# Attention with relative tables: where a head's value-table work, its key-table layout and its row copies stand

## The chip, the cores and the metric

The kernel runs on one core of one Trainium2 chip. The metric is the time of one execution in microseconds on the device; the median of several executions counts. TensorE, VectorE, ScalarE, GpSimd and SyncE each have an instruction stream of their own and meet through semaphores; in the views they are PE (PEld for its weight loads), DVE, ACT, POOL and SP. SPq, ACTq and POOLq are DMA issues by those engines.

## What is computed

The reference is two layers of a network on `x` of shape (4, 384, 32, 32): attention and a feed-forward with factored weights, then depthwise convolutions and a mixture of four experts. Everything is fp32. The change lies in the attention of the first layer, 8 heads of 48 features over 1024 pixels and 4 images:

```
attn = q @ k.T                                        # q is scaled, (b, h, 1024, 1024)
attn = attn + take(q @ table_k.T, idx)                # idx[i, j]: clipped (dy, dx) of pixels i and j, 15 x 15
attn = attn + take((k * scale) @ table_q.T, idx).T
attn = softmax(attn)
out  = attn @ v
wsum[i, idx[i, j]] += attn[i, j]                      # sums of the weights by offset
out  = out + wsum @ table_v
out  = out @ w_proj + b_proj
```

## The kernel before

**Stages.** A first phase normalises `x` and writes queries, keys and values to DRAM (to about 240 us of the span), the attention phase runs the 8 heads one after another (to about 1560 us), and a third phase does all the rest (to 3159 us). Only the attention phase is touched. Its matmuls, copies and DMAs are pinned: each engine executes them in the order in which the Python program writes them down.

**One head** consists of two parts.

*Tables.* `prepare` multiplies keys with `table_q` (tile `tabq_ps`) and queries with `table_k` (`tabk_ps`), one product of 128 x 480 for each of 32 columns of the image (480 is 15 row offsets by 32). A step handles two columns of each, the `tabq` columns four ahead of the `tabk` columns, so there are 18 steps a head. ACT copies each `tabq` product from PSUM (L314) and SP writes it to the DRAM tile `sd` (L220), from which SP loads it back transposed (`s1`; the views call it `s`). DVE transposes each `tabk` product in blocks of 32 x 32 from PSUM into `b2` (L309). `b2` is laid out `[offset, y, x]`, so a transposed column lands in words that lie 32 words (128 bytes) apart. Six steps of the next head's tables run during the last two rows of a head and after them; the other twelve follow before the head's first row.

*Rows.* For each of 32 image rows y (one row of all four images is 128 queries, by 1024 keys):

- `fetch` (L352): POOL adds `b2` and `s1` into a tile `bias` of 128 x 1024 by up to three additions; three such tiles exist. Row pairs of `s1` come by one DMA of 480 KB; two such tiles exist.
- `scores`: 16 matmuls into one of two PSUM tiles (`sc_ps`).
- `biased` (L380): DVE adds scores and bias, and takes the row minimum. It frees the `sc_ps` tile.
- `exponentials` (L390): ACT, with the row sums.
- `far_sums` (L401): three DVE reductions for the offsets beyond the window.
- `transposes` (L409): 8 on PE, and two ACT copies (L410) into `aT`.
- `windows` (L419): 4 transposes on PE; `keep_windows` (L428) copies their 128 x 512 result into `a1t`. Odd y and y = 16 are copied by ACT, the others by DVE: 17 and 15 of 32.
- after each four rows, `values`: 64 matmuls (`av_ps`) and one ACT copy (L443).

Scores run three rows ahead of the transposes, `biased` two, `far_sums` one.

*Value table.* After rows 15 and 31, `wsum @ table_v` is computed in four quarters: `value_table(g)`, 64 matmuls with weights from `tvw` and data from `a1t` into one PSUM bank (`tv_ps`), then `add_table` (L478), four DVE additions onto the head's output `o`. The quarters for rows 16 to 31 of a head stand at the start of the next head: after its first two scores come quarters 0 and 1 with their additions, then the matmuls of quarter 2, `biased` and `exponentials` of row 0, the addition and the matmuls that are left, scores of row 2, and so on (L530 to L546). `tvw` for the next use is loaded by 15 DMAs of 192 KB, one a row from row 1, and the values `vb` by 4 DMAs of 256 KB at rows 0 to 3; both are issued by ACT (`bulk`, L223), in order with its copies and exponentials. Queries (`qs`), `s1`, `sd` and the softmax denominators (`rb`) are DMAs of SP (`dma`, L220). Besides the bias, POOL scales the finished output of a half head (L490), once at each of the rows 4, 8, 20 and 24.

## Time and profile before

| | |
|---|---|
| median of 3 runs | 3158.37 us (3157.34 to 3163.52) |
| profiled execution, its own time | 3161.11 us |
| its span, first to last instruction | 3159.3 us, granted PE clock 0.970 |
| busy PE / DVE / ACT / POOL | 2975.0 / 2000.4 / 1331.1 / 1157.8 us |
| attention, first `biased` of head 4 to that of head 5 | 938.72 to 1101.99 us |

In the views, a line of a group gives source line, engine, operation, output and input tiles, shapes and count, then the busy time and the mean ns of one, then the idle time of the engine just before them and what ended it. A line of a timeline gives start, length, engine, source line and count of merged instructions, and in brackets the idle time before them. A line of a window gives the stretch, then the busy time of PE, PEld, DVE, ACT and POOL (with counts), the granted PE clock as a share of full speed, the DMA share and GB/s.

### The profile page before, as it was taken

The numbers are of one execution on the slowest core, as the hardware profiler recorded it, in microseconds if no ns is written. First come the engines' busy times: TensorE is split into PE (matmuls) and PEld (weight loads), VectorE is DVE, ScalarE is ACT, GpSimd is POOL, SyncE is SP. The second block draws the span as 40 slices with busy tenths as digits, with TensorE's granted clock in tenths as the row PEclk, the third lists the DMA queues.
The fourth block names the chain that finished last, engine by engine and source line by source line (L and its number), as shares of the span: only waits on it lengthen the run. The fifth ranks groups of instructions, "written<-read, shape, count | busy, mean of one in ns | idle before, by whom it ended". The sixth has DMA issues, their size and how long they took to land.

```text
span 3159.3 us, 63461 instructions
## 1 busy us (share of the span) xinstructions
PE 2975.0 (94%) x25591; PEld 2061.6 (65%) x25591; DVE 2000.4 (63%) x3739; ACT 1331.1 (42%) x2695; POOL 1157.8 (37%) x1100
## 2 busy tenths in 40 slices
PE   8998999999999999999878997998999999999996
PEld 4545766667676767676633374674677777778775
DVE  2227777877788787877649399998999720001101
ACT  1105656565656566565420332342342423333332
POOL 2224637372737372737410221113135232114422
PEclk9999999999999999999989998998999999999998
DMA  3796465555555555555331322351355044475852
GB/s 126 262 313 208 126 187 138 182 135 168 147 173 148 179 141 185 142 176 155 96 112 44 128 71 110 147 206 53 127 191 189 28 174 172 155 283 173 309 206 73
DMA packets 263669, 500.53 MB, mean 158 GB/s; under 512 B 135200, under 2 KB 188064, under 8 KB 255696
## 3 DMA queue, kind: packets, MB, share of 16 engines
q1 hardware_dynamic: 156528, 214.73, 21.4%
q0 software_dynamic: 43552, 228.24, 19.6%
q10 hardware_dynamic: 63296, 53.52, 7.2%
q8 instruction: 201, 3.29, 0.4%
q14 instruction: 92, 0.75, 0.1%
HBM read 543.58 MB, written 152.37 MB: 220 GB/s over the span
## 4 chain that ended last, share of the span: by engine, by line
PE 37%; DVE 10%; issue 4%; DMA 2%; ACT 1%; POOL 1%; POOLq 0%; ACTq 0%; DVEq 0%; SPq 0%
PE e_ps L1226 14%; PE y_ps L1204 14%; DVE xb L1021 7%; PE av_ps L215 1%; PE row_ps L75 1%; PE tap_ps L1065 1%; PE o_ps L966 1%; PE t_ps L409 1%; PE all_ps L105 1%; PE proj_ps L931 1%; PE xT_ps L1188 1%; PE sc_ps L215 1%; PE f_ps L962 1%; PE tv_ps L215 0%; PE u_ps L949 0%
## 5 line engine op out<-in xcount | busy, mean ns | idle before, releaser
L352 POOL TENSOR_TENSOR bias<-b,s 128x416 f32<-128x416 f32 (+24 forms) x656 | 660.4, 1045 | 525.8 <-DMA s<-sd 434.9
L1226 PEld LDWEIGHTS e_ps<-xT,w 128*128 128x128 f32 x4824 | 654.6, 193 | 229.7 <-ACT hs L972 16.1
L1226 PE MATMUL e_ps<-xT,w 128*128 128x128 f32 x4824 | 673.3, 277 | 19.8 <-DVE xb L934 8.0
L1204 PE MATMUL y_ps<-w,eh 128*128 128x384 f32 x1608 | 651.0, 490 | 6.2 <-ACT eh L1229 6.2
L1021 DVE SCALAR_TENSOR_TENSOR xb<-img,c_w,xb 128x1024 f32<-128x1024 f32 (+1 forms) x539 | 610.2, 1189 | 0.0
L1229 ACT ACTIVATE eh<-e_ps,w 128x128 f32<-128x128 f32 x804 | 294.1, 368 | 740.7 <-PE e_ps L1226 728.1
L1194 POOL DMA_INDIRECT w<-in_w,row x134 | 163.5, 1220 | 773.5 <-PE y_ps L1204 266.5
L401 DVE TENSOR_REDUCE extra<-arow 128x32 f32<-128x32 f32 (+24 forms) x768 | 380.7, 556 | 3.3 <-ACT arow L390 2.9
L390 ACT ACTIVATE arow<-arow,nm 128x1024 f32<-128x1024 f32 x256 | 297.9, 1164 | 143.0 <-DVE nm L380 135.8
L409 PEld LDWEIGHTS t_ps<-ident,arow 128*128 128x128 f32 x2048 | 223.9, 143 | 193.0 <-DVE a1t L428 68.1
L380 DVE CUSTOM_DVE_ANT_0 arow<-sc_ps,bias 128x1024 f32<-128x1024 f32 x256 | 312.2, 1220 | 35.2 <-issue 21.0
L410 ACT COPY aT<-t_ps 128x512 f32<-128x512 f32 x512 | 277.1, 594 | 134.7 <-PE t_ps L409 129.6
L1207 DVE TENSOR_TENSOR yo<-y_ps,w 128x384 f32<-128x384 f32 x67 | 37.1, 553 | 442.0 <-PE y_ps L1204 442.0
L215 PE MATMUL sc_ps<-kk,qs 48*32 48x512 f32 x4096 | 289.3, 623 | 25.4 <-DVE nm L380 23.1
L409 PE MATMUL t_ps<-ident,arow 128*128 128x128 f32 x2048 | 287.4, 284 | 13.4 <-DVE a1t L428 12.2
L215 PEld LDWEIGHTS av_ps<-aT,vb 128*64 128x64 f32 x4096 | 224.4, 137 | 56.9 <-ACT aT L410 46.9
L1204 PEld LDWEIGHTS y_ps<-w,eh 128*128 128x128 f32 x1608 | 248.2, 193 | 18.6 <-ACT eh L1229 7.8
L309 DVE STREAM_TRANSPOSE b<-tabk_ps 128x480 f32<-128x480 f32 x256 | 216.1, 1006 | 49.3 <-PE tabk_ps L215 35.7
L215 PE MATMUL av_ps<-aT,vb 128*64 128x128 f32 x4096 | 241.0, 275 | 4.6 <-DMA vb<-v_d 4.6
L215 PE MATMUL tabq_ps<-tab,kq 48*128 48x480 f32 x512 | 220.3, 579 | 2.1 <-ACT aT L410 1.4
L215 PE MATMUL tabk_ps<-tab,kq 48*128 48x480 f32 x512 | 219.3, 579 | 1.0 <-DVE b L309 1.0
L314 ACT COPY st<-tabq_ps 128x480 f32<-128x480 f32 x256 | 142.4, 561 | 74.4 <-PE tabq_ps L215 38.7
(212 smaller groups left out, 3199.4 us busy)
## 6 DMA issues: line engine op xcount, KB each, us to landing
sd<-st SPq DMA_DIRECT2D x128, 480.0 KB, 2.5
s<-sd SPq DMA_DIRECT2D x128, 480.0 KB, 4.4
xs_d<-zero POOLq DMA_DIRECT2D x8, 3072.0 KB, 12.7
tvw<-in_tv ACTq DMA_DIRECT2D x120, 192.0 KB, 3.3
y_d<-yo SPq DMA_DIRECT2D x67, 192.0 KB, 1.9
qk_d<-qk_sb POOLq DMA_DIRECT2D x48, 256.0 KB, 5.5
qs<-qk_d SPq DMA_DIRECT2D x256, 48.0 KB, 2.9
kq<-qk_d ACTq DMA_DIRECT2D x56, 192.0 KB, 3.9
```

What stands on the lines that cost most here:

```text
L215: ins = nc.tensor.matmul(*args, **kw)
L309: turn = nc.vector.transpose(b2.rearrange("p e y x -> p x (e y)")[:, i + j], ps[:, j, : SPAN * IMG])
L352: nc.gpsimd.tensor_tensor(bias[:, y0:y1, :], bass.AP(b2.tensor, b2.offset + (e * IMG + y0) * IMG, [list(b2.ap[0]), [(step * IMG + 1) * IMG ...
L380: nc.vector.tensor_tensor_reduce(s["flat"], ps.rearrange("p h n -> p (h n)"), s["bias"].rearrange("p y x -> p (y x)"), -SCALE, BIG, ALU.ad ...
L390: nc.scalar.activation(s["flat"], s["flat"], AF.Exp, bias=s["nm"], scale=-1.0, accum_out=dn[:, y % YT : y % YT + 1])
L401: pin(nc.vector.tensor_reduce(ex[:, i, :], a[:, p0:p1, :].rearrange("p y x -> p x y"), AX.X, ALU.add))
L409: pin(nc.tensor.transpose(pt[:, j, :], s["flat"][:, k0 : k0 + P], ident))
L410: pin(nc.scalar.copy(aT[:, 4 * g : 4 * g + 4, s["y"] % YB, :], pt))
L1021: nc.vector.scalar_tensor_tensor(acc[:, k, y0:y1], img[:, k, dy + y0 : dy + y1, dx : dx + IMG], w7[:, k, dy, dx : dx + 1], acc[:, k, y0:y1 ...
L1204: nc.tensor.matmul(py, hs, w[:, o : o + C], start=(ff == 0), stop=(ff == NF - 1))
L1226: nc.tensor.matmul(ph, w[:, o : o + P], xT[k][:, c, :], start=(c == 0), stop=(c == KC - 1))
L1229: nc.scalar.activation(hs, ph, AF.Gelu, bias=w[:, o : o + 1])
```

## The change

1. `b2` holds each transposed column as 480 consecutive words, columns 481 words apart. DVE now writes consecutive words; POOL, which read runs of consecutive words, now reads words that lie 481 words (1924 bytes) apart.
2. Value-table quarter 0 moves into the tables of the next head, behind the eighth of the twelve remaining steps. Quarters 1, 2 and 3 stand before, between and after the scores of rows 0 and 1. The PSUM pools of the quarters are swapped.
3. `vb` is loaded during the tables; it is still issued by ACT. `tvw` is issued by SP.
4. The first row pair of `s1` comes as two DMAs of one row each.
5. ACT copies all `a1t` rows but those with y mod 16 of 8 or 12: 28 of 32.
6. Rows 0 to 2 are ordered anew: scores and `biased` run less far ahead at first, and `windows` of row 0 waits until row 1. Rows from 3 on are as before.

```diff
-        b2 = fixed.tile([P, SPAN, IMG, IMG], F32, name="b2")
+        b2 = fixed.tile([P, IMG * PITCH], F32, name="b2")          # PITCH = SPAN * IMG + 1
                         turn = nc.vector.transpose(
-                            b2.rearrange("p e y x -> p x (e y)")[:, i + j], ps[:, j, : SPAN * IMG]
+                            b2[:, (i + j) * PITCH : (i + j) * PITCH + SPAN * IMG], ps[:, j, : SPAN * IMG]
                         )
...
+                for r, n in ((0, 2),) if y else ((0, 1), (1, 1)):
+                    dma(
+                        rows[0][:, r : r + n].rearrange("p r e x -> p r (e x)"),
...
-                            b2.tensor, b2.offset + (e * IMG + y0) * IMG,
-                            [list(b2.ap[0]), [(step * IMG + 1) * IMG, n], [1, IMG]],
+                            b2.tensor, b2.offset + e * IMG + y0,
+                            [list(b2.ap[0]), [step * IMG + 1, n], [PITCH, IMG]],
...
-            copy = nc.scalar.copy if y % 2 or y == YT else nc.vector.tensor_copy
+            copy = nc.vector.tensor_copy if y % YT in (8, 12) else nc.scalar.copy
...
-            pool, tag = (ps_o, "o") if g % 2 else (ps_t, "t")
+            pool, tag = (ps_o, "o") if g % 2 != other else (ps_t, "t")
...
-                bulk(
+                dma(
                     tvw[p : p + IMG, i // 4].rearrange("p i d -> p (i d)"),
...
-            for _ in tables:
+            parts, pieces = load_values(h), load_value_table(h)
+            for i, _ in enumerate(tables):
+                next(parts, None)
+                if n and i == 7:
+                    add_table(batch[1], 0, value_table(0, 1))
+            for _ in parts:
                 pass
             for s in blk[:3]:
                 fetch(s)
-            parts, pieces = load_values(h), load_value_table(h)
+            if n:
+                po = value_table(1, 1)
             scores(blk[0])
+            if n:
+                add_table(batch[1], 1, po)
+                po = value_table(2, 1)
             scores(blk[1])
             if n:
-                for g in range(2):
-                    add_table(batch[1], g, value_table(g))
-                po = value_table(2)
+                add_table(batch[1], 2, po)
+                po = value_table(3, 1)
             biased(blk[0])
             exponentials(blk[0])
             if n:
-                add_table(batch[1], 2, po)
-                po = value_table(3)
-            scores(blk[2])
+                add_table(batch[1], 3, po)
+            biased(blk[1])
             far_sums(blk[0])
-            biased(blk[1])
-            exponentials(blk[1])
-            if n:
-                add_table(batch[1], 3, po)
...
                 transposes(s)
-                windows(s)
-                if y == 0:
-                    scores(blk[3])
+                if y < 3:
+                    exponentials(blk[y + 1])
+                    if y == 0:
+                        scores(blk[2])
+                    if y == 1:
+                        windows(blk[0])
+                    scores(blk[y + 3])
+                    biased(blk[y + 2])
+                    far_sums(blk[y + 1])
+                    if y == 1:
+                        keep_windows(blk[0])
+                if y:
+                    windows(s)
```

## The prediction

> **What bounds it now.** I read the page first, then the timeline of the start of head 5, then windows over it, then groups by form for prices. The page's busy line and two DVE and POOL groups:

> ```profile
> PE 2975.0 (94%) x25591; PEld 2061.6 (65%) x25591; DVE 2000.4 (63%) x3739; ACT 1331.1 (42%) x2695; POOL 1157.8 (37%) x1100
> L309 DVE STREAM_TRANSPOSE b<-tabk_ps 128x480 f32<-128x480 f32 x256 | 216.1, 1006 | 49.3 <-PE tabk_ps L215 35.7 <-PE tabq_ps L215 13.5
> ```

> PE is busy nearly always, so only what PE waits for can be won, unless PE work goes away, and none does. In the rows of a head from the first `av` on PE repeats 2.48, 2.62, 2.75 and 6.12 us from scores to scores, against 2.48, 2.48, 2.48 and 6.12 in its best groups: some 0.4 us in 14. In the tables a step's products follow each other every 0.81 us on PE and `st` copies on ACT do the same; DVE needs 0.845 per transpose, a lag of 0.8 us over 24 that PE never feels (PE waits 1.0 us for L309 in the whole run). So the tables are PE's. What is left is the start of a head. Timeline, head 5, from the end of its tables:

> ```profile
> 1094.07 0.88 SPq L220 DMA_DIRECT2D s<-sd  x2
> 1094.15 1.09 PE L215 MATMUL sc_ps<-kk,qs 48*32 48x512 f32 x16
> ...
> 1096.52 7.59 PE L215 MATMUL tv_ps<-a1t,tvw 128*48 128x64 f32 x256
> ...
> 1098.03 12.40 POOL L352 TENSOR_TENSOR bias<-b,s 128x224 f32<-128x224 f32 x10 [49.72 <-DMA s<-sd]
> 1098.63 1.58 DVE L478 TENSOR_TENSOR oT<-tv_ps,oT 48x128 f32<-48x128 f32 x4 [3.19 <-issue]
> ...
> 1101.99 1.23 DVE L380 CUSTOM_DVE_ANT_0 arow<-sc_ps,bias 128x1024 f32<-128x1024 f32 x1
> ...
> 1107.87 1.09 PE L215 MATMUL sc_ps<-kk,qs 48*32 48x512 f32 x16 [0.94 <-DVE nm L380]
> ...
> 1110.64 1.96 PE L215 MATMUL sc_ps<-kk,qs 48*32 48x512 f32 x16 [1.69 <-DVE nm L380]
> ...
> 1112.13 0.68 DVE L428 COPY a1t<-a_ps 128x512 f32<-128x512 f32 x1
> ```

> The reader is to see that DVE starts 4.5 us after the tables end and is then busy without a gap, and that PE twice waits for `biased` to free a score tile. The windows show a second loss:

> ```profile
> 1106.00:1110.00 4.00, 1.90 (x22) 0.57 (x20) 3.88 (x9) 2.15 (x4) 4.00 (x4) 1.00 0.21 51
> 1110.00:1114.00 4.00, 3.36 (x23) 1.70 (x24) 4.00 (x10) 1.60 (x4) 2.95 (x3) 0.50 0.62 138
> ```

> PE is under half busy, and then its clock is granted at 0.50. DVE, not PE, is late there, so this costs little now. The first `av` (rows 0 to 3 are through) starts 27.8 us after the tables' end in head 5; over heads 1 to 7 the mean is 27.9, in head 0 it is 23.2 and the `av` is cut by a wait for `vb`.

> **Part 2 and 6, the start.** I lay the new DVE order over the durations of this timeline, T = 0 at the end of the tables. A quarter's matmuls take 7.6/4 = 1.9 us, 16 scores 1.05, an addition of a quarter 1.6, `biased` 1.15 until the next DVE instruction, `far_sums` 1.75 falling to 1.55.
> PE: quarter 1 to 1.9, scores 0 to 2.95, quarter 2 to 4.9, scores 1 to 5.95, quarter 3 to 7.9. DVE: addition 1 from 2.1 to 3.7, addition 2 from 5.05 to 6.7. Bias of row 0: the `s` DMA is issued at 0 as now; now it lands after 3.96 us, 480 KB at the 300 GB/s of this phase are 1.6 us, so half of it (part 4) saves 0.8, POOL starts at 3.2 and needs 2.6 a row (660 us over 256 rows): ready at 5.8. So `biased` 0 starts at 6.75, with addition 2 last, then without a gap addition 3, `biased` 1 at 9.45, 2 at 12.3, 3 at 15.1, 4 at 17.75, 5 at 20.4, done 21.6. ACT keeps pace: exponentials 0 end at 9.3, 1 at 12.4, 2 at 15.5, 3 at 19.0, each needed by DVE or PE no earlier. Scores 7 wait for `biased` 5 and end at 22.7; the first `av` starts there. Quarter 0 went ahead of T: plus 1.9 PE. 27.9 − 22.7 − 1.9 = 3.3 us a head, **23 us** for 7 heads. The gain is DVE's: addition 0 (1.6) and two row copies (0.7 each) leave this stretch.
> Quarter 0 in the tables: PE pauses 1.9 us there, DVE adds for 1.6, so DVE's lag doesn't grow, and two score tiles hold four transposes. Uncovered it would cost the 1.6.
> Head 0 has no quarters. `biased` 0 comes 0.8 us sooner, POOL still paces rows 1 and 2, two row copies leave DVE: scores of row 7 about 1.5 us sooner; and `av` no longer waits for `vb` (scores 7 to scores 8 take 10.3 us there instead of 6.1): **5.6 us**. Heads 1 and 2 show the same wait with 0.9 each: **1.8**.

> **Part 3.** `vb` in the tables: ACT has 0.25 us free between copies, an issue takes 0.33, four steps later it is caught up. 1 MB more among 480 KB each 1.62 us: 736 KB a step ask for 450 GB/s where 419 is the most that the DMA view shows in a slice (head 0's tables), so `sd` falls back by some 0.6 us and has eight steps to catch up. Zero, with 0.6 a head if not. `tvw`: 15 issues of 0.33 leave ACT (5.0 us a head) and stand in SP's queue behind `qs` and `s1`; needed at row 16, the last is issued at row 15, lands after 3.3. Queued behind it on SP: `s1` of the next pair, needed two rows later. Zero.

> **Part 5.** 11 copies a head at 0.585 go to ACT: 6.4 us, 1.4 net of `tvw`. DVE loses 11 of 0.68. PE's 0.4 us in 14 is half a wait for DVE's copies (L409 on L428, at y = 11 0.7 us), and an ACT copy stands behind a 1.2 us exponential: rows 4 to 15 gain some 0.2 a group, rows 17 to 31, where `tvw` was not, lose 0.2 to 0.3. Zero, ends −1 and +1 us a head.

> **Part 1.** Two prices. DVE's transpose becomes shorter: nearest rows, 1006 ns now, and 691 ns for 128x512 of consecutive words (L167): 0 to −0.35 us each. It buys nothing, as DVE is not late in the tables. POOL reads one of its two inputs at a step of 1924 bytes; the trace has no such POOL row:

> ```profile
> L352 POOL TENSOR_TENSOR bias<-b,s 128x416 f32<-128x416 f32 x176 | 189.6, 1082 | 126.6 <-DMA s<-sd 98.1 <-DVE nm L380 18.7 <-DVE extra L401 9.7
> L352 POOL TENSOR_TENSOR bias<-b,s 128x800 f32<-128x800 f32 x16 | 30.4, 1898 | 0.0
> L1047 POOL TENSOR_TENSOR w<-half,c_w 128x3136 f32<-128x3136 f32 x2 | 10.8, 5445 | 10.8 <-DVE b_first L808 10.8
> L401 DVE TENSOR_REDUCE extra<-arow 128x32 f32<-128x800 f32 x16 | 25.1, 1569 | 1.2 <-ACT arow L390 1.2
> L401 DVE TENSOR_REDUCE extra<-arow 128x32 f32<-128x512 f32 x16 | 17.4, 1087 | 0.0
> ```

> POOL pays (1898 − 1082)/384 = 2.13 ns per element; with inputs that repeat one word (L1047) 1.74. So its pattern matters: −0.4 us a row of 1024 at one end. DVE reading at a step of 128 bytes pays (1569 − 1087)/288 = 1.67, and on consecutive words (1220 for 1024, 691 for 512) 1.03: +0.64 ns, +0.65 us a row at the other. POOL is already slower per element than DVE's stepped read, so part may hide: I take +0.3. Bias 5 is ready at 3.2 + 6 × 2.9 = 20.6 where it is wanted at 20.4: **0 to 0.2 us**. At +0.65 it is 22.6, a loss of 2.2 a head, 18 in all. Later rows give POOL 14 us for four rows and at most one L490 of 1.3: 4 × 2.9 + 1.3 = 12.9 fits.
> [...]

> **The clock.** PE's waits in the new start are 7.9 to 9.3, then 0.1 to 0.65 at a time: in the worst 3.4 us PE is some 58% busy, where 48% (1.90 of 4.00) was followed by the halved clock. If it comes, transposes 0, scores 2 and 3 take 6 us instead of 3 and `biased` 2 starts 1.1 late. I count 1.1 in each of 7 heads: **−7.7**.
> [...]

> **Sum.** 23 + 5.6 + 1.8 − 7.7 = 22.7 us. Profiled execution 3161.1 − 22.7 = 3138.4; it lies 2.7 above the median of the runs shown, so 3136 for a median.

> **Rivals.** *The start stays late* (22%). One of half-rate clock over two windows, `vb` delaying `sd`, or ACT's copies costs 2 us a head more: 3136 + 16 = 3152. For it: the 0.50 lasts 6.8 us in heads 3 to 7. Against: DVE, not PE, is the chain there.
> *POOL becomes the bound* (15%), slower than before. If the column read costs +1.0 us a row (2.13 to 3.1 ns), bias 5 is ready at 24.7, 4.3 late; four rows and L490 need 15.6 of 14 us, 1.6 too much at rows 4 and 8 and 0.35 in other groups, some 3.6 until the pause at row 16. 7.9 us × 8 = 63, less the 30 won (the halved clock is covered): 3158 + 33 = 3191. POOL decides the start from +0.28 on ((20.4 − 3.2)/6 − 2.58), and the total is zero near +0.75. For it: L1047 against L352. Against: DVE's stepped price is +0.65 at most.
> *It does nothing* (3%): if `biased` 0 waited for a late `s`, as now, order on DVE would not matter: 3158.

> **Numbers.** Forecast 3136, 60%, own range 3120 to 3150 (all clocks kept and rows +1 us: −16; POOL at +0.65: +14). Range for 8 in 10: 3120 to 3168, which takes in the late start and the foot of the POOL case. The measurement tells 0.2% (6.3 us) from no change: faster is 60 + half of 22, 0.71; same 11 + 3, 0.14; slower 0.15.

> **What would show it.** Right: first `av` some 22.7 us after the tables' end; no gap on DVE from `biased` 0 to 5; PE's longest wait at `transposes` of row 0; L352 at 128x800 near 2.1 us; L309 shorter without effect. Wrong: L352 at 128x800 above 2.5 us with DVE waiting for POOL; ACT as what L409 or L419 waits for; clock 0.50 for 6.8 us in all heads; a longer pitch of `st` copies while `vb` loads.

## The result and the profile after

The changed kernel takes 3158.47 us (median of 20 runs, 3153.56 to 3164.56), the kernel before 3160.37 us (20 runs on the same chip, 3151.43 to 3170.66): a ratio of 0.9993 with an interval of 0.9983 to 1.0002, so no change. The forecast was 3136 us. The profiled execution took 3161.57 us, with a span of 3159.8 us and a granted PE clock of 0.973.

The page after, its busy line and the key column's transposes (columns as before):

```profile
PE 2972.0 (94%) x25591; PEld 2036.6 (64%) x25591; DVE 1915.7 (61%) x3651; ACT 1363.1 (43%) x2783; POOL 1288.8 (41%) x1100
L310 DVE STREAM_TRANSPOSE b<-tabk_ps 128x480 f32<-128x480 f32 x256 | 173.3, 681 | 117.5 <-PE tabk_ps L216 77.9 <-PE tabq_ps L216 17.6
```

DVE lost 85 us of work and POOL gained 131, and PE is as busy as it was. DVE now waits 77.9 us for PE in the tables, where it waited 35.7: the table steps come later than they did. The start of head 5, in the timeline after, from the end of its tables at 1101.36:

```profile
1101.42 1.27 SPq L221 DMA_DIRECT2D s<-sd  x3
1103.23 1.09 PE L216 MATMUL sc_ps<-kk,qs 48*32 48x512 f32 x16
...
1104.15 18.05 POOL L354 TENSOR_TENSOR bias<-b,s 128x224 f32<-128x224 f32 x12 [52.50 <-DMA s<-sd]
...
1106.30 1.59 DVE L480 TENSOR_TENSOR oT<-tv_ps,oT 48x128 f32<-48x128 f32 x4 [1.40 <-PE tv_ps L216]
1107.93 1.23 DVE L382 CUSTOM_DVE_ANT_0 arow<-sc_ps,bias 128x1024 f32<-128x1024 f32 x1
...
1110.49 1.09 PE L411 MATMUL t_ps<-ident,arow 128*128 128x128 f32 x8 [1.28 <-ACT arow L392]
...
1110.88 1.22 DVE L382 CUSTOM_DVE_ANT_0 arow<-sc_ps,bias 128x1024 f32<-128x1024 f32 x1
...
1120.67 1.09 PE L216 MATMUL sc_ps<-kk,qs 48*32 48x512 f32 x16 [0.81 <-DVE nm L382]
```

This is the start that was laid out: `biased` of row 0 at 6.6 us after the tables, of row 1 at 9.5, PE's longest wait at the transposes of row 0, and no gap on DVE. Windows over the end of the same head's tables, after, and before at the same place in the steps (us; busy PE, PEld, DVE, ACT, POOL; PE clock, DMA share, GB/s):

```profile
1078.00:1082.00 4.00, 4.00 (x22) 3.02 (x20) 3.37 (x6) 2.50 (x5) 0.00 (x0) 1.00 0.90 315
1082.00:1086.00 4.00, 2.61 (x14) 1.57 (x12) 1.94 (x3) 1.02 (x2) 0.00 (x0) 1.00 0.99 381
1086.00:1090.00 4.00, 4.00 (x13) 1.68 (x12) 2.05 (x3) 2.14 (x4) 0.00 (x0) 0.55 0.67 274
1090.00:1094.00 4.00, 4.00 (x56) 2.26 (x54) 1.37 (x2) 1.12 (x2) 0.00 (x0) 0.60 0.40 166
```

```profile
1075.00:1079.00 4.00, 4.00 (x22) 3.09 (x21) 3.54 (x5) 2.59 (x5) 0.00 (x0) 1.00 0.32 125
1079.00:1083.00 4.00, 4.00 (x24) 3.35 (x22) 4.00 (x6) 2.75 (x6) 0.00 (x0) 1.00 0.75 301
1083.00:1087.00 4.00, 4.00 (x23) 3.83 (x21) 4.00 (x6) 2.76 (x6) 0.00 (x0) 1.00 0.78 313
```

In these windows PE was busy throughout before, and the DMA engines were 0.78 full at most. After, they are full, PE stands still for a third of a window, and then its clock is granted at about half. The timeline of the same stretch tells why PE stood still:

```profile
1076.20 0.35 ACTq L224 DMA_DIRECT2D vb<-v_d  x1
1076.77 16.31 SPq L221 DMA_DIRECT2D sd<-st  x8
...
1077.81 0.34 ACTq L224 DMA_DIRECT2D vb<-v_d  x1
...
1079.42 0.33 ACTq L224 DMA_DIRECT2D vb<-v_d  x1
1080.72 0.56 ACT L315 COPY st<-tabq_ps 128x480 f32<-128x480 f32 x1 [0.74 <-DMA sd<-st]
1081.04 0.33 ACTq L224 DMA_DIRECT2D vb<-v_d  x1
1081.17 0.56 ACT L315 COPY st<-tabq_ps 128x480 f32<-128x480 f32 x1
...
1084.21 1.02 ACT L315 COPY st<-tabq_ps 128x480 f32<-128x480 f32 x2 [2.47 <-DMA sd<-st]
1086.36 1.02 ACT L315 COPY st<-tabq_ps 128x480 f32<-128x480 f32 x2 [1.14 <-DMA sd<-st]
```

After the third load of `vb`, ACT's copy waits for a write of `sd` to free one of the three `st` tiles, first 0.74 us, then 2.47; PE then waits for ACT. The writes are late: before, a write of `sd` in these tables landed 2.5 us after its issue; here the writes issued at 1076.77, 1078.39 and 1081.76 took 3.9, 5.7 and 6.3 us. From 420 to 1450 us of the span, the waits of the changed kernel for this chain (total, times, longest) are:

```profile
ACT st L315 <- DMA sd<-st: 33.4, 25, 3.1
PEld tabq_ps L216 <- ACT st L315: 25.4, 27, 2.8
PE tabq_ps L216 <- ACT st L315: 12.0, 9, 2.1
```

Before, ACT waited 2.6 us there. A ledger from the two traces follows, with a head cut into tables (start of the last `av` product of a head to the end of the next head's `tabk` products, mean of 7), start (to its first `av`, mean of heads 1 to 7) and rows (start of the first to start of the last `av`, mean of heads 1 to 6):

| us | tables | start | rows | sum | end of head 0's tables to last `av` |
|---|---|---|---|---|---|
| before | 20.28 | 27.86 | 116.04 | 164.2 | 1283.7 |
| after | 26.38 | 23.84 | 115.06 | 165.3 | 1285.9 |

The starts won 7 × 4.0 = 28 us, the tables lost 7 × 6.1 = 43, and the rows with head 0 won 12. Outside of this the two traces agree: to 0.4 us at the end of head 0's tables, and to 2.2 us from the last `av` to the end.

### The profile page after: what moved, and what is told of

Read it like the earlier page. It is cut to its first block, busy times and chain, and to the rows that moved or that the text cites. A ratio compares the mean times of both kernels' runs of the same rounds, so it can differ in the third digit from the quotient of the medians.

```text
span 3159.8 us, 63493 instructions
## 1 busy us (share of the span) xinstructions
PE 2972.0 (94%) x25591; PEld 2036.6 (64%) x25591; DVE 1915.7 (61%) x3651; ACT 1363.1 (43%) x2783; POOL 1288.8 (41%) x1100
## 4 chain that ended last, share of the span: by engine, by line
PE 70%; DVE 11%; issue 6%; DMA 6%; POOL 4%; ACT 2%; SPq 0%; ACTq 0%; POOLq 0%; DVEq 0%
PE e_ps L1244 14%; PE y_ps L1222 14%; PE t_ps L411 7%; PE av_ps L216 7%; DVE xb L1039 7%; PE sc_ps L216 6%; PE tabq_ps L216 5%; PE a_ps L421 3%; POOL bias L354 3%; PE qk_ps L164 2%; DMA sd<-st 2%; PE tv_ps L216 2%; DMA s<-sd 1%; PE row_ps L76 1%; PE v_ps L175 1%
## 5 line engine op out<-in xcount | busy, mean ns | idle before, releaser
L354 POOL TENSOR_TENSOR bias<-b,s 128x416 f32<-128x416 f32 (+24 forms) x656 | 793.3, 1278 | 443.6 <-DMA s<-sd 332.9
L382 DVE CUSTOM_DVE_ANT_0 arow<-sc_ps,bias 128x1024 f32<-128x1024 f32 x256 | 312.1, 1219 | 116.3 <-POOL bias L354 59.8
L411 PE MATMUL t_ps<-ident,arow 128*128 128x128 f32 x2048 | 281.0, 280 | 18.6 <-ACT arow L392 17.6
L216 PE MATMUL sc_ps<-kk,qs 48*32 48x512 f32 x4096 | 278.2, 603 | 12.8 <-DVE nm L382 12.1
L216 PE MATMUL tabq_ps<-tab,kq 48*128 48x480 f32 x512 | 238.9, 613 | 19.2 <-ACT st L315 17.0
L310 DVE STREAM_TRANSPOSE b<-tabk_ps 128x480 f32<-128x480 f32 x256 | 173.3, 681 | 117.5 <-PE tabk_ps L216 77.9
L216 PE MATMUL tabk_ps<-tab,kq 48*128 48x480 f32 x512 | 236.3, 610 | 0.0
L216 PEld LDWEIGHTS tabq_ps<-tab,kq 48*128 48x128 f32 x512 | 147.7, 298 | 84.1 <-ACT st L315 33.1
```

The costliest lines, as they stand in the source:

```text
L216: ins = nc.tensor.matmul(*args, **kw)
L310: turn = nc.vector.transpose(b2[:, (i + j) * PITCH : (i + j) * PITCH + SPAN * IMG], ps[:, j, : SPAN * IMG])
L354: nc.gpsimd.tensor_tensor(bias[:, y0:y1, :], bass.AP(b2.tensor, b2.offset + e * IMG + y0, [list(b2.ap[0]), [step * IMG + 1, n], [PITCH, IMG]],
L382: nc.vector.tensor_tensor_reduce(s["flat"], ps.rearrange("p h n -> p (h n)"), s["bias"].rearrange("p y x -> p (y x)"), -SCALE, BIG, ALU.ad ...
L411: pin(nc.tensor.transpose(pt[:, j, :], s["flat"][:, k0 : k0 + P], ident))
```

## The experiments

Two theories at first. **V**: the loads of `vb` in the tables fill the DMA engines, `sd` is late, ACT and PE wait, the clock halves. **P**: POOL's read at a step takes the gain back. All ratios are against the kernel before in the same group of runs on the same chip. The columns of the ledger are those above, from one execution of each run. That execution lies between 6.5 us below the median of its run (e8) and 7.2 us above (e4), and the stretch behind the attention, which no edit touches, differs by up to 8 us between runs of one chip. So the columns tell where time goes, and the ratios what it is worth.

| run | ratio and interval | tables | start | rows | sum | attention |
|---|---|---|---|---|---|---|
| e1 loads at the rows | 0.9960 [0.9943, 0.9978] | 22.37 | 23.66 | 116.58 | 162.6 | 1265.4 |
| e2 loads spread in the tables | 0.9995 [0.9982, 1.0008] | 22.93 | 24.93 | 115.05 | 162.9 | 1270.7 |
| e3 old layout | 0.9998 [0.9984, 1.0013] | 26.06 | 22.90 | 114.75 | 163.7 | 1275.0 |
| e4 before, loads in the tables | 1.0047 [1.0028, 1.0065] | 23.04 | 27.68 | 115.62 | 166.3 | 1295.3 |
| e5 = e1, old layout | 0.9955 [0.9937, 0.9972] | 23.07 | 23.27 | 115.88 | 162.2 | 1263.7 |
| e7 = e5, old copies | 0.9963 [0.9948, 0.9979] | 23.05 | 24.98 | 114.93 | 163.0 | 1270.8 |
| e8 = e1, two loads a row | 0.9960 [0.9945, 0.9975] | 22.35 | 25.17 | 115.05 | 162.6 | 1266.6 |
| e9 = e1, quarter 0 after | 0.9940 [0.9917, 0.9963] | 20.18 | 24.85 | 116.15 | 161.2 | 1258.5 |
| e13 quarter 0 after | 0.9973 [0.9961, 0.9985] | 23.31 | 25.16 | 114.82 | 163.3 | 1274.1 |
| e10 = e9, old layout | 0.9916 [0.9903, 0.9930] | 20.37 | 24.67 | 116.15 | 161.2 | 1257.1 |
| e11 = e9, loads a row sooner | 0.9912 [0.9898, 0.9925] | 20.20 | 24.97 | 115.82 | 161.0 | 1256.2 |
| e12 = e11, old layout | 0.9889 [0.9874, 0.9904] | 20.30 | 24.71 | 115.39 | 160.4 | 1249.3 |

**e1 and e4: the loads.** e1 is the changed kernel with the loads back at rows 0 to 3:

```diff
             for i, _ in enumerate(tables):
-                next(parts, None)
...
-            for _ in parts:
-                pass
...
                 if y + 3 < IMG:
                     fetch(blk[y + 3])
+                next(parts, None)
```

> The changed kernel with one part undone: the four loads of the values stand at rows 0 to 3 of a head again, still issued by ACT. Theory V (the loads fill the DMA engines during the tables, the sd writes fall behind, ACT and then PE wait, PE's clock halves): the tables of heads 1 to 7 lose their 4 us each, some 28 us, and 3 to 6 us come back as waits for the values in heads 0 to 2: 3134 to 3140 us, ratio to before 0.992 to 0.994, st copies 0.81 us apart throughout. Rival P (POOL's column read takes what the new start gives): within 3 us of the changed kernel, ratio 0.998 to 1.000.

e4 makes the opposite edit in the kernel before, and nothing else:

> The kernel before with one part of the change alone: the four loads of the values stand behind the table steps instead of at rows 0 to 3 (there six of 18 steps of head 0, and the first four of the last twelve of the others). Theory V: 4 us a head lost in the tables of 7 heads, 4 to 6 us won by the waits for the values in heads 0 to 2: 3178 to 3186, ratio 1.006 to 1.009. Rival P: the waits for the values go and nothing else changes, ratio 0.998 to 0.999.

ACT's wait for `sd` in the same stretch of the span is gone in e1, and is there in e4 without any other part of the change:

```profile
ACT st L315 <- DMA sd<-st: 2.9, 2, 1.6
```

```profile
ACT st L314 <- DMA sd<-st: 29.0, 25, 2.8
```

The tables fall by 4.0 us in e1 and rise by 2.8 in e4. V holds in both directions. That ACT issues the loads between its copies is not the cause: in the trace after its copies start every 0.81 us up to the third issue, and what ends its waits is a write of `sd`; and e2 below has the same issues with tables as short as e1's to 0.6 us. By time e4 lies below V's range, with an interval that reaches into it, and e1 lies between the two expectations: part of the 28 us comes back as waits for `vb` at row 4 (rows 1.5 us longer than after), and e1's tables are still 2.1 us longer than before, which is quarter 0.

**e2 and e3: spreading the loads, and the old layout alone.** e2 issues the four loads at every third step; e3 undoes the layout of `b2` in the changed kernel.

```diff
-                next(parts, None)
+                if i % 3 == 0:
+                    next(parts, None)
```

```diff
-        b2 = fixed.tile([P, IMG * PITCH], F32, name="b2")
+        b2 = fixed.tile([P, SPAN, IMG, IMG], F32, name="b2")
...
-                            b2[:, (i + j) * PITCH : (i + j) * PITCH + SPAN * IMG], ps[:, j, : SPAN * IMG]
+                            b2.rearrange("p e y x -> p x (e y)")[:, i + j], ps[:, j, : SPAN * IMG]
...
-                            [list(b2.ap[0]), [step * IMG + 1, n], [PITCH, IMG]],
+                            [list(b2.ap[0]), [(step * IMG + 1) * IMG, n], [1, IMG]],
```

> The changed kernel with the four loads of the values spread over the tables: at the first, fourth, seventh and tenth of the twelve steps instead of the first four. Theory V as a burst: 256 KB more in every third step ask for some 355 GB/s, below what the DMA engines gave (381), so the copies keep to 0.81 us and the run comes to 3132 to 3140, ratio 0.991 to 0.994. V without burst (any megabyte more is too much): ratio 0.996 to 1.000, the late steps stretched instead of the middle ones. Rival P: ratio 0.998 to 1.000.

> The changed kernel with one part undone: the key table keeps its old layout, so DVE writes words 128 bytes apart and POOL reads runs of consecutive words. Theory V: tables as in the changed kernel, POOL back to 2.58 us a row, the starts some 1 us a head shorter: 3148 to 3156, ratio 0.996 to 0.999. Rival P: DVE waited 52 us for POOL's bias in the changed kernel against 13 before; with them gone some 30 us or more are won, 3120 to 3130, ratio 0.988 to 0.991.

e2's tables are nearly cured (22.93), but its starts are 1.3 us longer than e1's: POOL's first bias of a head begins 4.5 us after the tables in place of 3.2. Part of the delay was moved to the first fetch, and by the ratio the kernel is still no faster than before, though its one traced execution, 5.6 us below the median, has an attention 13 us shorter than before. P falls with e3: POOL is back at its old price (12 additions at the start of head 5 take 14.9 us, 18.1 in the changed kernel; 10 took 12.4 before) and the starts are 0.9 us shorter, but the tables are nearly as long as after, and the time is the same. (The attention of the traced execution is 10.9 us shorter than after; of these, 7.4 are the distances of the two executions from their medians.)

**e5, e7, e8, e9: each other part, with the loads out of the tables.** e5 is e1 with e3's edit. e7 adds to it the first edit here; e8 is e1 with the second:

```diff
-            copy = nc.vector.tensor_copy if y % YT in (8, 12) else nc.scalar.copy
+            copy = nc.scalar.copy if y % 2 or y == YT else nc.vector.tensor_copy
```

```diff
-                next(parts, None)
+                if y < 2:
+                    next(parts, None)
+                    next(parts, None)
```

> The changed kernel with the values loaded at rows 0 to 3 again and the key column's table in its old order, so that DVE's transposes write with a step and POOL reads contiguously. The trace of the run with the new order and the loads at the rows gave, a head, a start 4.2 us shorter than before, tables 2.3 us longer (the quarter) and rows as long. Theory N (the new order buys nothing, its price on POOL is paid in the starts): a start some 0.8 us shorter still, as in the run with the old order alone (22.9 against 23.8 us), so a ratio of 0.992 to 0.995. Theory L (the shorter transposes make room on DVE for the quarter's adds among the tables, without them the twelve steps stretch): twelve steps of 19 us or more, ratio 0.997 to 1.000.

> As the run beside it, and with the copies of the row offsets shared between ScalarE and VectorE as before the change: what is left is the new order of a head's start, with quarter 0 among the tables, the first fetch in two parts and the pieces of the value table on SP. Theory S (the start is the whole gain, the copies are worth nothing, as the prediction took it): the same as the run with all copies on ScalarE within 0.002, that is 0.992 to 0.997. Theory C (the copies carry the rows: 114.7 to 115.0 us a head with them, 115.6 without, in the runs so far, and VectorE is freed for the start): 6 us and more lost against that run, ratio higher by 0.002 to 0.005.

> The changed kernel with the values loaded two at row 0 and two at row 1, in place of one at each of the rows 0 to 3. In the run with one a row, TensorE waited 13 us in all for these loads at the first values of a head, and the rows were 116 to 119 us long in place of 115. Theory V (the loads must only be clear of the tables and early enough for row 4): no wait for them is left, rows of 115 us, some 1.2 us a head less, ratio 0.992 to 0.995. Rival F (two loads at a row delay the fetch of the next rows' offsets, and POOL's bias with it, in the start, which is bound by them): starts of 24.5 us or more, ratio 0.997 to 1.000.

> The changed kernel with the values loaded at rows 0 to 3 and with quarter 0 of the value table after the tables again, ahead of quarter 1, not among them. Theory Z (the quarter is only moved: it took 2.24 us of the tables' pitch and frees 1.9 us and more of the start): tables of 15.4 us, starts 2 to 2.5 us longer, no difference by time within 0.0015 to the run with the quarter among the tables (0.996). Theory Q (the quarter in the tables is a gain, as the prediction took it: TensorE works there while the key column's transposes are behind): 0.998 to 1.000. Theory H (it does harm, the pause of the pitch delays the last steps and the first fetch): 0.992 to 0.994.

e5: the old layout does no harm without the loads (0.9955 against 0.9960, intervals overlap); the tables are 0.7 us longer and the starts 0.4 shorter, so neither N's gain nor L's loss is seen by time. e7: by the ratio the copies are worth 0.0008, inside the intervals, as S has it; by the medians it is 6.9 us and by the attention of the traces 7.1, in the starts (25.0 against 23.3) and not in the rows. That is open. e8: the wait for `vb` is gone and the rows are 115.05, but the start is 1.5 us longer, and from 420 to 1450 us of the span DVE waits 60.0 us for POOL's bias, 52.5 in e1, which is what F expects; the two cancel. e9 is e1 with the edit

```diff
-                if n and i == 7:
-                    add_table(batch[1], 0, value_table(0, 1))
...
-                po = value_table(1, 1)
+                p0, po = value_table(0, 1), value_table(1, 1)
...
+                add_table(batch[1], 0, p0)
```

and is the fastest of its group (3172.63 us against 3176.84 to 3183.69 of the other three). By the ledger the quarter cost the tables 2.2 us and took only 1.2 off the start, a harm of 1 us a head, as H has it; whether by H's mechanism isn't shown, and the interval of the time takes in Z as well.

**e13, e10, e11, e12: the square, and the best version.** The same edit in the changed kernel itself, with the loads still in the tables, is e13; e11 (from e9) and e12 (from e9 with the old layout, which is e10) issue the loads by

```diff
-                next(parts, None)
+                for _ in range((1, 2, 1)[y] if y < 3 else 0):
+                    next(parts, None)
```

> The changed kernel with one thing undone: quarter 0 of the value table is computed after the tables, not among them; the values are still loaded in the tables. With the run that undid the loads alone (0.996) and the run that undid both (0.994) it makes a square of two by two. Theory V (the loads in the tables are by themselves the loss, about 4 us a head, and the quarter is another 1 us): the stretch from a head's last values to the end of the next key table 24 to 24.5 us (26.4 in the changed kernel, 20.2 with both undone), the start 24.8, 1 us a head won, ratio 0.996 to 0.998. Theory I (the two together are worse than the sum: the quarter's 2.2 us of pause leaves the loads and the table's writes a longer queue, and TensorE a quiet stretch that halves its clock): the stretch 23 us as in the run of before with the loads alone, ratio 0.993 to 0.995.

> The best version so far (values at rows 0 to 3, quarter 0 after the tables: 0.994) with the key column's table in its old order. Theory N (the new order is a price on POOL and no gain without the quarter in the tables): starts of 23.9 to 24.3 us in place of 24.85, the stretch before them 20.2 to 20.4 us, ratio 0.992 to 0.994. Theory L (the new order's shorter transposes are needed): the stretch 21 us and more, ratio 0.995 or above.

> The best version so far (values at rows 0 to 3, quarter 0 after the tables) with the values at rows 0, 1, 1 and 2. In its trace TensorE waited 13 us in all for the third image's values, which had been issued 7 us ahead of their use and the fourth's 4 us ahead. Theory V: the wait goes, rows of 115.0 in place of 116.1 us, starts of 24.85 to 25 us, ratio 0.992 to 0.994. Rival F (the loads delay the row offsets that the start waits for, as two a row at rows 0 and 1 did, where the start was 25.2 in place of 23.7 us): starts of 25.8 us or more, ratio 0.994 to 0.996.

> Both at once: quarter 0 after the tables, the values at rows 0, 1, 1 and 2, the key column's table in its old order. If both are gains by their own theories they add: starts of 24 us, rows of 115 us, the stretch before 20.3 us, 159.3 us a head against 164.2 in the kernel before, 5 us a head, ratio 0.989 to 0.992. If the loads and the faster POOL meet (POOL then waits for the offsets that the loads delay), no more than the better of the two, 0.993.

By time the square adds up: with the quarter after the tables the loads cost 0.9973 − 0.9940 = 0.0033, with the quarter among them 0.9993 − 0.9960 = 0.0033, some 10 us each, give or take 8 and 6; the quarter costs 0.002 in both, clear of the noise with the loads in the tables (e13), inside it without (e9). The ledgers of single executions put the loads higher, at 15.6 and 20.5 us of attention. Theory I saw the tables rightly (23.3 us) and V the time; that the two together are worse than their sum is not shown. ACT's wait for `sd` is 31.0 us in e13, as in the changed kernel, so it does not need the quarter.

In e9 the wait that was left at the first values was this (the expectations of e8 and e11 add up the two lines and say 13 us, but they show the same waits twice, at the weights and at the products; PE's line alone is 5.8 us, and 6.1 in e1):

```profile
PEld av_ps L216 <- DMA vb<-v_d: 7.3, 6, 2.0
PE av_ps L216 <- DMA vb<-v_d: 5.8, 6, 1.8
```

With the loads at rows 0, 1, 1 and 2 no such wait is left. e12 takes 3124.53 us against 3159.73 of the kernel before, 35 us less; e11 and e10 in the same group 3132.23 and 3133.56. Each gains by time what was expected or a little more, but not where: the starts stay at 24.7 to 25.0 with either layout, where 24 was expected of the old, and e11's rows are 115.8 in place of 115.0. In e12 no half-rate clock is left in heads 1 to 7 (granted clock over the span 0.978, before 0.970), ACT waits 2.3 us for `sd`, and the groups of POOL and of the transposes are those of before:

```profile
PE 2955.1 (95%) x25591; PEld 2049.0 (66%) x25591; DVE 1954.9 (63%) x3651; ACT 1364.0 (44%) x2783; POOL 1154.1 (37%) x1100
L310 DVE STREAM_TRANSPOSE b<-tabk_ps 128x480 f32<-128x480 f32 x256 | 217.1, 997 | 56.1 <-PE tabk_ps L216 36.0 <-PE tabq_ps L216 20.2
L354 POOL TENSOR_TENSOR bias<-b,s 128x416 f32<-128x416 f32 x176 | 190.0, 1085 | 104.4 <-DMA s<-sd 82.8 <-DVE extra L403 15.4 <-DVE nm L382 6.3
```

So the version that beats both keeps the new order of the start, the copies on ScalarE, the split first fetch and `tvw` on SP, and gives up the new layout, the quarter among the tables and the loads in them. No run undoes the new order of the start, the split fetch or `tvw` on SP alone, so what each of them is worth stays open. A second tile for `vb`, filled during the rows of the head before, would need neither place; it wasn't tried.

## Why the prediction was wrong

**Part 3 failed**, where it said that "`sd` falls back by some 0.6 us and has eight steps to catch up. Zero, with 0.6 a head if not." It put the loads at nothing, or 0.6 us a head. They cost 4.0 us of tables a head (after against e1), 28 us in 7 heads; the other pairs of runs say 2.8 (e4 against before), 3.0 (e3 against e5) and 3.1 (e13 against e9). After what they spare at row 4 it is about 20 us in these traces and some 10 by the ratios. The sum had 736 KB a step against 419 GB/s, a peak from another stretch; here the engines were full (0.99) at 381 GB/s, in a window in which PE waited. Two things were not priced. First, being late is felt at once: three `st` tiles let ACT run only so far ahead of `sd`, and PE only the three `tabq_ps` tiles ahead of ACT. Second, PE's wait was followed by the half clock. The heads of the after trace sort by it: tables of 24.0 and 25.2 us with no half-rate time in them, 25.9 and 26.4 with 3.4 us of it, 27.4, 27.6 and 28.1 with 6.8. Against e1's 22.4 the late writes alone are 2.2 us a head, and each 3.4 us of half rate goes with some 1.6 more. The list of what would show it wrong had the sign ("a longer pitch of `st` copies while `vb` loads"), and the rival of the late start named the cause, at half the size and in the wrong place.

**Part 2 and 6, the start: right in its order, and in its sum by luck.** First `av` at 22.7 us after the tables was predicted, 23.8 measured, 22.9 with the old layout (e3). `biased` of rows 0 to 5 was laid at 6.75, 9.45, 12.3, 15.1, 17.75 and 20.4; the medians of heads 1 to 7 are 6.6, 9.6, 12.6, 15.4, 18.3 and 21.3 after, and 6.5, 9.5, 12.4, 15.1, 17.9 and 20.6 in e3. With the half clock it charged, the prediction counted 36.4 − 7.7 = 28.7 us off the seven starts; 28.1 came. The two agree by luck: the 7.7 for the clock was not lost, and POOL's read, put at 0 to 0.2 us, took 0.9 of each start (after against e3), 6.6 in all. And 1.9 of each was the quarter's move, which the prediction expected the tables to pay with as much; they pay 2.1 (e1 against before), and by the ledger it is a net loss of 1 us a head (e1 against e9): without it the tables are 2.2 us shorter and the start only 1.2 longer. From `biased` 0 to 5 it is 14.1 us there and 14.6 in e1, which is 0.4 of the difference; the rest is not explained. Head 0 won 3.9 in place of 5.6; e1 wins 4.3 there with the loads at the rows, so their new place was not needed for it.

**Part 1, POOL: mis-sized, and worth little.** A row takes 793.3/256 = 3.10 us in place of 660.4/256 = 2.58, +0.52 where +0.3 was taken. The groups after:

```profile
L354 POOL TENSOR_TENSOR bias<-b,s 128x416 f32<-128x416 f32 x176 | 231.9, 1326 | 39.0 <-DMA s<-sd 32.9 <-DVE nm L382 6.0
L354 POOL TENSOR_TENSOR bias<-b,s 128x800 f32<-128x800 f32 x16 | 37.2, 2326 | 0.0
L382 DVE CUSTOM_DVE_ANT_0 arow<-sc_ps,bias 128x1024 f32<-128x1024 f32 x256 | 312.1, 1219 | 116.3 <-POOL bias L354 59.8 <-issue 54.4 <-PE sc_ps L216 0.7
```

(2326 − 1326)/384 is 2.60 ns an element against 2.13: the prediction's sign of trouble, L352 at 128x800 above 2.5 us, was not reached, yet DVE now waits 59.8 us for POOL, 13.5 before. Of that, 0.4 to 0.9 us a head reaches the start (e1 against e5, after against e3). By time the whole layout costs 3132.23 − 3124.53 = 7.7 us in e11 against e12, on one chip, and nothing that shows in after against e3 or e1 against e5. The transposes became 0.33 us shorter, and the prediction put the worth of that at nothing; without the loads the tables are 0.1 to 0.7 us a head shorter with them (e11 against e12, e9 against e10, e1 against e5), which the starts lose again in part (e1 against e5: 0.4).

**Part 5: not settled, within its ends of 1 us a head.** e7 is 6.9 us slower than e5 by the medians, 0.0008 by the ratio, with intervals that overlap.

**The clock: wrong place.** The starts of heads 1 to 7 had 44 us of half rate before and have none after, so the 7.7 was not lost there; the tables had none and have 27 us.

**The sum.** Predicted: starts 28.7, quarter −13.3, waits for `vb` 1.8, head 0 5.6, together 22.8. Measured by the ledger: starts 28.1, tables −42.7, of which the quarter is about −14.6 and the loads −28.1, rows of heads 1 to 7 +8.5, head 0 +3.9, together −2.2. With the loads at the rows (e1) the trace wins 18.3 us and the time 12.8 by its ratio (0.9960, the interval from 7 to 18): the starts win 29.4, the quarter costs 14.6, head 0 wins 4.3, and the waits at row 4 take back what the rows had won. So without the loads in the tables most of the forecast 22 us is there. The range, 3120 to 3168, takes the time in at the end that was added for the rivals. One rival, that it does nothing, had named 3158, but for a cause that did not come: `biased` 0 was to wait for a late `s`, and it started at 6.6 us, as laid out.

## What to carry to other kernels

- A transfer that is moved must be priced in the stretch it is moved to, against the rate that this stretch itself shows when full, and with the number of buffers that stand between the DMA queue and the engine that sets the pace: here, with three of them, ACT's first wait came 3.8 us, less than three steps, after the first load was issued.
- Work that is moved under a phase bound by TensorE is not hidden, it is added; it must take as much off the phase it leaves, and here the start gave back 1.2 us for the 2.2 that the tables paid.
- When a change does several things and the time stands still, cut the time into phases in both traces first. Here 28 us won and 43 us lost stood side by side, and undoing three of the parts left 35 us (e12).
